# First weights held until the first tokens are normalised, the MLP's transposes spread between its last additions, and twice the buffers for its output rows

## The chip, the cores and the metric

The kernel runs on one core of one Trainium2 chip. The metric is the device time of one execution in microseconds (us), lower is better; the median of several runs is compared. The engines are TensorE (PE in the profile; PEld is its loading of weights), VectorE (DVE), ScalarE (ACT), GpSimd (POOL) and SyncE (SP), which issues the transfers (DMAs).

## The reference, cut to what matters

The input is one image of 48 x 48 positions ("tokens", 2304 in all) with 768 channels, float32. Two layers follow each other:

```python
# layer 0: a transformer block
xn  = layernorm(x);  q, k, v = xn @ qkv_w + qkv_b        # 12 heads of 64
attn = softmax(q k^T * scale + rel_h + rel_w);  x = x + (attn v) @ proj_w + proj_b
h = gelu(layernorm(x) @ mlp_w1 + mlp_b1);  x = x + h @ mlp_w2 + mlp_b2   # 768 -> 3072 -> 768
# layer 1: a spectral filter
xf = rfft2(x);  o = two small complex matrix products per frequency, 8 channel blocks of 96
x = irfft2(softshrink(...)) + x
```

## The kernel before, in words

Everything is float32. A tile of tokens is 128 tokens x 768 channels, so there are 18 tiles. The order of the work on TensorE is written out by hand in the kernel (`manual_schedule`), and in the first stage that of SyncE's transfers too; on VectorE, ScalarE and GpSimd a scheduler orders the instructions when the kernel is built, and each engine then works through its list in that order. Large matrix products are made by Strassen's scheme with seven products for eight, so there are sums of blocks of weights (`left` and `right`, on GpSimd, lines L152 to L161) and of tokens (`sums_of_tokens`, four subtractions on VectorE, L170).

**The start.** `queries_keys_values` works in three blocks of six tiles. For the first block, `arrive` issues six loads of tokens (L373, 384 KB each, 128 rows of 3,072 B), `normal` normalises each tile (`normalise`: two statistics L116, their combination L118, a square root on ScalarE L120, a reciprocal L121 and the scaling L124). Then `weights_of` issues the first two pairs of weights, two loads each (L357, 384 KB each in pieces of 512 B), and `left` prepares them on GpSimd. `channels_first` transposes the tiles on TensorE (L386) and reads the results by VectorE (L389) and ScalarE (L393) into the token block `xt`; `sums_of_tokens` makes `xs`; then the products of L429 begin.

**The MLP.** It goes through three blocks `p` of 768 tokens. For each block, twelve steps `n` make 256 hidden channels each (`hidden`, products of L958, Gelu L964, then the sums `hs` on VectorE, L152 to L155) and add their share of the output (`added`, products of L1022 and L1018 into the four banks `o0` to `o3`, each read at once by VectorE into `x1` or `acc`, L1026, L1020, L1034). `added` of step n runs between the parts of `hidden` of step n + 1; the last step's three additions stand alone. While a block is worked on, the next block's tiles are normalised into `hats` (`normalised`). At the boundary of two blocks the kernel calls `turned`, which transposes the six normalised tiles of the next block (L1069, 36 transposes into the banks `h0` to `h3`, three to a bank) and reads the twelve filled banks into `xt`, by ScalarE (L1072) and VectorE (L1076) in turn. Then come the last three additions with `sums_of_tokens` cut in pieces between them, and `rows_forward`.

**From the MLP to the spectral stage.** `rows_forward(p)` multiplies the finished rows by a Fourier matrix (L1045, 16 results `zp` in the banks `o0` to `o3`), copies each into a buffer `zt` by ScalarE and VectorE in turn (`balanced_copy`, L75 and L77; four buffers), and writes each to memory (L1051). After the third block the spectral stage loads its first frequencies `zi` (L914) and starts with the products `fp` (L1168), whose banks are those that `zp` had, and whose results `xf` are copied by L75 and L77 in turn.

Of the kernel before, what the change touches and what calls it, by code (L numbers as in the profile page):

```python
# [18 lines left out]
P = 128  # L19
# [4 lines left out]
NC = C // P  # L24
# [5 lines left out]
G = 384  # L30
NB = 8
BS = C // NB
CH = C // 2
KW = HW // 2 + 1
# [5 lines left out]
V_LN1G, V_LN1B, V_LN2G, V_LN2B, V_QB, V_KB, V_VB, V_B1 = 0, 6, 12, 18, 24, 30, 36, 42  # L40
# [4 lines left out]
def block_then_afno(  # L45
# [25 lines left out]
    nc = tc.nc  # L71

    def balanced_copy(i, dst, src):
        if i % 2:
            nc.scalar.copy(dst, src)  # L75
        else:
            nc.vector.tensor_copy(dst, src)  # L77
# [11 lines left out]
    def col(i):  # L89
        return vec[:, i : i + 1]  # L90
# [18 lines left out]
    xt = shared[:, : NC * TB].rearrange("p (c t) -> p c t", c=NC)  # L109
    xs = shared[:, NC * TB :].rearrange("p (k c t) -> p k c t", k=3, c=3)  # L110

    def normalise(pool, src, hat=None):

        stats = pool.tile([P, 2, 6], F32, name="stats")
        for i in range(2):
            nc.vector.bn_stats(stats[:, i, :], src[:, ts(i, C // 2)])  # L116
# [7 lines left out]
        nc.vector.tensor_scalar(hat, src, mv[:, 0:1], rstd, ALU.subtract, ALU.mult)  # L124
        return hat

    def transposed(psum, hats, dst, g, gcol, bcol, tag):
# [35 lines left out]
    def sums_of_tokens(xt, xs, piece=None):  # L163

        b11, b12, b21, b22 = (xt[:, ds(3 * i, 3), ts(j, G)] for i in range(2) for j in range(2))
        t1, t2, t4 = (xs[:, i] for i in range(3))
        steps = ((t1, b12, b11), (t2, b22, t1), (t4, b21, t2), (b12, b22, b12))
        for i, (dst, a, b) in enumerate(steps):
            if piece is None or piece == min(i, 2):
                nc.vector.tensor_tensor(dst, a, b, ALU.subtract)  # L170
# [16 lines left out]
    with ExitStack() as flag_scope:  # L187
# [11 lines left out]
        with ExitStack() as att:  # L199
# [115 lines left out]
            def queries_keys_values(qkv):  # L315
# [35 lines left out]
                        [wvs[:, i] for i in range(3)],  # L351
                    )

                def weights_of(pr, slot):
                    w, ws = pairs[slot]
                    for i in range(2):
                        nc.sync.dma_start(  # L357
                            out=w[:, :, i],
                            in_=qkv_w[:, ds(i * C + pr * P, P)].rearrange("(c p) f -> p c f", p=P),
                        )  # L360
                    left(
                        nc.gpsimd, w[:, 0:3, 0], w[:, 3:6, 0], w[:, 0:3, 1], w[:, 3:6, 1],
                        [ws[:, i] for i in range(3)],
                    )
                    return w, ws
# [3 lines left out]
                def arrive(g):  # L369
# [3 lines left out]
                        nc.sync.dma_start(out=x3[:, i], in_=blocks[g, i])  # L373
                    arrived[g] = x3

                def normal(t):
                    x3 = arrived[t // 3]
                    normalise(ln1, x3[:, t % 3], x3[:, t % 3])

                def channels_first(g):  # L380
                    x3 = arrived[g]
# [103 lines left out]
                    orders.append(work)  # L485

                pairs_left = [i for work in orders for kind, i in work if kind == 0]
                ahead = [weights_of(pairs_left.pop(0), i) for i in range(2)]
                slot = 0
                for p in range(T // TB):  # L490
                    for g in (2 * p, 2 * p + 1):
# [426 lines left out]
    with ExitStack() as mlp:  # L918
# [81 lines left out]
        def added(p, n, i):  # L1000

            h, hs, v, vs = kept[p, n]
            bank = [psum.tile([P, CH], F32, name=f"o{k}") for k in range(4)]
            if n == 0:
                acc[i] = upool.tile([P, CH], F32, name=f"acc{i}", bufs=1)
            a11, a12, s3, a22 = (
                h[:, f, ds(k * G + i * P, P)] for f, k in ((0, 0), (1, 0), (0, 1), (1, 1))
            )
            s1, s2, s4 = (hs[:, k, ts(i, P)] for k in range(3))
            b11, t3, b21, b22 = (v[:, f, ts(k, CH)] for f in range(2) for k in range(2))  # L1010
            t1, t2, t4 = (vs[:, k] for k in range(3))
            t = 2 * (p * 3) + i
            x11, x12, x21, x22 = (
                x1[:, t + 3 * j, ts(k, CH)] for j in range(2) for k in range(2)
            )

            def product(k, a, b, start, *into):
                nc.tensor.matmul(bank[k], a, b, start=start, stop=True, skip_group_check=not start)  # L1018
                for dst in into:
                    nc.vector.tensor_tensor(dst, bank[k], dst, ALU.add)  # L1020

            nc.tensor.matmul(bank[0], a11, b11, start=True, stop=True)  # L1022
            if n == 0:
                nc.vector.tensor_copy(acc[i], bank[0])
            else:
                nc.vector.tensor_tensor(acc[i], bank[0], acc[i], ALU.add)  # L1026
            product(1, s2, t2, True, acc[i])
            product(2, s3, t3, True, x22)
            product(3, s1, t1, True, x22)
            product(0, a12, b21, False, x11)  # L1030
            product(2, a22, t4, False, x21)
            product(3, s4, b22, False, x12)
            if n == n_f - 1:
                nc.vector.tensor_tensor(x21, x21, acc[i], ALU.add)  # L1034
                nc.gpsimd.tensor_tensor(x12, x12, acc[i], ALU.add)
                nc.gpsimd.tensor_tensor(x22, x22, acc[i], ALU.add)

        def rows_forward(p):

            for k in range(2):  # L1040
                for g in (2 * p, 2 * p + 1):
                    for a, parts in enumerate(((0,), (1, 2), (3, 4), (5,))):
                        zp = psum.tile([2 * 2 * KW, CH], F32, name="zp", tag=f"o{a}")
                        for b in parts:
                            nc.tensor.matmul(  # L1045
                                zp, rows_dft[:, b, :], x1[:, 3 * g + b // 2, ts(k, CH)],
                                start=(b == parts[0]), stop=(b == parts[-1]),
                            )
# [8 lines left out]
        def normalised(p, i):  # L1057

            t = 6 * p + i
            hats[i] = turn.tile([P, C], F32, name="hat2", tag="turn")  # L1060
            normalise(upool, x1[:, t, :], hats[i])
            nc.gpsimd.tensor_tensor(x1[:, t, :], x1[:, t, :], b2, ALU.add)

        def turned():
            for j in range(2):
                for c in range(NC):
                    tp = psum.tile([P, G], F32, name="tp2", tag=f"h{c % 4}")
                    for i in range(3):
                        nc.tensor.transpose(tp[:, ts(i, P)], hats[3 * j + i][:, ts(c, P)], ident)  # L1069
                    dst = xt[:, c, ts(j, G)]  # L1070
                    if c % 2:
                        nc.scalar.activation(  # L1072
                            dst, tp, AF.Identity, bias=col(V_LN2B + c), scale=col(V_LN2G + c)
                        )
                    else:
                        nc.vector.tensor_scalar(  # L1076
                            dst, tp, col(V_LN2G + c), col(V_LN2B + c), ALU.mult, ALU.add
                        )

        with tc.manual_schedule(engines={mybir.EngineType.PE}):  # L1080
            for p in range(T // TB):
                for n in range(n_f):
                    work = hidden(p, n)
                    for i in range(3):
                        next(work)
                        if n:
                            added(p, n - 1, i)
                    if p < 2 and 4 <= n < 10:
                        normalised(p + 1, n - 4)
                if p < 2:  # L1090
                    turned()
                for i in range(3):
# [315 lines left out]
```

## Time and profile before

| What | Value |
|---|---|
| Median of three runs | 2972.0 us (2969.34, 2972.0, 2973.16) |
| The profiled execution's own time | 2968.75 us |
| Its span in the profile | 2966.9 us |
| TensorE busy | 2901.3 us, 98% of the span |
| VectorE, ScalarE, GpSimd busy | 60%, 29%, 21% |
| TensorE's clock granted, mean | 0.996 of full speed |
| From the first transposes to `rows_forward`, first boundary | 1964.03 to 1990.45 us |
| The same, second boundary | 2317.47 to 2342.52 us |
| `rows_forward` of the third block | from 2684.73 us |
| First `fp` | 2704.24 us |

All times of the profile are microseconds from the start of the span. The span leaves out what lies around the program, 1.85 us in this execution. A busy TensorE is one with matmuls in flight; the times of its matmuls are modelled at their ends. A row of the timeline gives start, length, engine, line, operation, what is written and read, how many instructions are merged, and in brackets how long the engine had been idle before and what ended that. A row of the windows gives the stretch, its length, the busy time of PE, PEld, DVE, ACT and POOL, the granted clock of TensorE, the mean busy share of the 16 DMA engines and the GB/s that they moved.

### The profile page before, as it was taken

To read this page: it belongs to the slowest core of one execution; us is meant where nothing else is said; L and a number is where in the kernel's file an instruction comes from. 1 tells how busy PE (TensorE), PEld (TensorE's weight loads), DVE (VectorE), ACT (ScalarE), POOL (GpSimd) and SP (SyncE) were. 2 spreads that over 40 slices of the span, in tenths; PEclk is the share of its full clock that TensorE was granted. 3 is DMA by queue.
4 is the path that set the end of the run, shared out by engine and by line. 5 is a ranking of instruction groups with operands and counts; after the bars stand their busy time and mean duration, and the time that the engine had idled before them with its cause. 6 is when DMAs were issued, how large, how long until landed. Compare 5 with 4: busy or idle time off the path is not lost. (4 is left out here: it accounts for less than half of the span.)

```text
span 2966.9 us, 40951 instructions
## 1 busy us (share of the span) xinstructions
PE 2901.3 (98%) x15771; PEld 1763.4 (59%) x15771; DVE 1779.2 (60%) x2576; ACT 867.4 (29%) x1344; POOL 609.4 (21%) x564
## 2 busy tenths in 40 slices
PE   6999999999999999999999999999999999999998
PEld 4555655655556555555555555555555555557995
DVE  4343237677777777777723666675666566664443
ACT  1011125655555556555500111011111111111210
POOL 2303010000000000000043332343233223312441
PEclk9999999999999999999999999999999999999999
DMA  4423276172452616435242021122112211213235
GB/s 118 152 87 115 94 161 125 26 135 57 83 123 42 141 33 104 103 58 87 62 166 85 32 64 54 54 70 64 51 62 64 75 44 64 64 57 88 78 89 177
DMA packets 202818, 253.04 MB, mean 85 GB/s; under 512 B 21618, under 2 KB 180978, under 8 KB 201078
## 3 DMA queue, kind: packets, MB, share of 16 engines
q1 hardware_dynamic: 202614, 250.32, 33.2%
q8 instruction: 127, 2.08, 0.3%
q14 instruction: 77, 0.63, 0.1%
HBM read 136.40 MB, written 50.14 MB: 63 GB/s over the span
## 5 line engine op out<-in xcount | busy, mean ns | idle before, releaser
L607 DVE TENSOR_TENSOR acc<-acc,main 128x768 f32<-128x768 f32 x576 | 551.8, 958 | 202.0 <-ACT main L550 145.4
L550 ACT ACTIVATE main<-sp 128x768 f32<-128x768 f32 x648 | 522.1, 811 | 155.8 <-PE sp L546 148.6
L546 PE MATMUL sp<-terms,select 64*128 64x384 f32 x1296 | 412.1, 629 | 0.0
L1020 DVE TENSOR_TENSOR main<-o,main 128x384 f32<-128x384 f32 x540 | 298.8, 556 | 40.3 <-PE o L1018 1.8
L958 PE MATMUL h<-shared,w 128*128 128x384 f32 x864 | 296.7, 486 | 0.8 <-issue 0.8
L540 PE MATMUL sp<-shared 64*128 64x384 f32 x1296 | 266.4, 488 | 2.8 <-DVE o L440 2.2
L540 PE MATMUL sp<-qT,kT 64*128 64x384 f32 x1296 | 266.5, 487 | 0.0
L585 POOL TENSOR_TENSOR inverse<-inverse,rden 128x384 f32<-128x384 f32 x36 | 46.3, 1287 | 1029.0 <-DVE rden L582 961.6
L429 PE MATMUL m<-main 128*128 128x384 f32 x756 | 247.1, 488 | 5.5 <-DVE rstd L121 2.6
L958 PEld LDWEIGHTS h<-shared,w 128*128 128x128 f32 x864 | 164.4, 190 | 116.1 <-issue 2.3
L958 PE MATMUL h<-shared,w1s 128*128 128x384 f32 x648 | 226.6, 486 | 0.0
L555 PE MATMUL op<-main,shared 128*64 128x384 f32 x1296 | 221.3, 488 | 0.0
L555 PE MATMUL op<-main,v 128*64 128x384 f32 x1296 | 219.9, 488 | 0.0
L429 PEld LDWEIGHTS m<-main 128*128 128x128 f32 x756 | 142.7, 190 | 107.5 <-issue 8.1
L964 ACT ACTIVATE hT<-c,vec 128x384 f32<-128x384 f32 x108 | 66.4, 615 | 466.2 <-DVE c L970 466.0
L970 DVE TENSOR_TENSOR c<-h,u 128x384 f32<-128x384 f32 x108 | 60.1, 557 | 212.4 <-PE h L958 212.4
L1018 PE MATMUL o<-w,hT 128*128 128x384 f32 x432 | 175.0, 487 | 2.2 <-DVE mv L118 2.0
L1018 PE MATMUL o<-w2s,hs 128*128 128x384 f32 x432 | 174.9, 487 | 1.1 <-DVE hs L153 1.1
L546 PEld LDWEIGHTS sp<-terms,select 64*128 64x128 f32 x1296 | 125.3, 186 | 83.8
L958 PEld LDWEIGHTS h<-shared,w1s 128*128 128x128 f32 x648 | 123.1, 190 | 85.9
L152 POOL TENSOR_TENSOR w1s<-w 128x384 f32<-128x384 f32 x36 | 36.2, 1005 | 611.7 <-PE o L1018 452.6
L555 PEld LDWEIGHTS op<-main,v 128*64 128x64 f32 x1296 | 89.9, 138 | 107.0 <-issue 107.0
(150 smaller groups left out, 3921.6 us busy)
## 6 DMA issues: line engine op xcount, KB each, us to landing
w<-in_mlp_w_dram SPq DMA_DIRECT2D x72, 768.0 KB
terms<-col_parts SPq DMA_DIRECT2D x432, 72.0 KB
terms<-row_hi SPq DMA_DIRECT2D x216, 72.0 KB
terms<-row_lo SPq DMA_DIRECT2D x216, 72.0 KB
main<-in_qkv_w_dram SPq DMA_DIRECT2D x36, 384.0 KB
z<-zt SPq DMA_DIRECT2D x48, 150.0 KB
zo<-z SPq DMA_DIRECT2D x12, 600.0 KB
x<-in_x_dram SPq DMA_DIRECT2D x18, 384.0 KB
```

Of the source, the lines that this page charges most:

```text
L429: nc.tensor.matmul(bank, a[:, c, :], b[:, c, :], start=(first and c == 0), stop=(c == 2), skip_group_check=not first,)
L540: nc.tensor.matmul(sp[:, j, :G], kT[at, ts(kt, P)], qT[at, ts(c, G)], start=True, stop=False,)
L546: nc.tensor.matmul(sp[:, j, :G], select[at, a % 2], ready[pr, c][at, a // 2, b], start=False, stop=True,)
L550: nc.scalar.activation(p, sp[:, :, :G], AF.Exp, scale=HD**-0.5)
L555: nc.tensor.matmul(op[ts(j, 64)], v[:, kt0 + i, ts(j, 64)], ps[i][:, j, :], start=(kt0 + i == 0), stop=(kt0 + i == NT - 1),)
L585: nc.gpsimd.tensor_tensor(inverse, inverse, rden, ALU.add)
L607: nc.vector.tensor_tensor(acc, made[0] if kt == 1 else acc, p, ALU.add)
L958: nc.tensor.matmul(bank[i], a[:, c, :], b[:, c, :], start=(start and c == 0), stop=(c == 2), skip_group_check=not start,)
L964: nc.scalar.activation(h[:, i, ts(k, G)], src, AF.Gelu, bias=col(V_B1 + 2 * n + i))
L970: nc.vector.tensor_tensor(t, src, other, ALU.add)
L1018: nc.tensor.matmul(bank[k], a, b, start=start, stop=True, skip_group_check=not start)
L1020: nc.vector.tensor_tensor(dst, bank[k], dst, ALU.add)
```

## The change

Three parts. First, `normalise` hands back its last instruction (the scaling), and each of the first four weight loads is made to wait for one: both loads of the first pair for that of tile 3, both of the second for that of tile 4. Second, `turned` is cut in three pieces of four banks, one ahead of each of the last three additions; all its reads are ScalarE's, and `sums_of_tokens` is called after the additions in one piece. Third, `zt` gets eight buffers for four, and for the first two blocks ScalarE makes all its copies.

```diff
-    def normalise(pool, src, hat=None):
+    def normalise(pool, src, hat=None, made=None):
...
-        nc.vector.tensor_scalar(hat, src, mv[:, 0:1], rstd, ALU.subtract, ALU.mult)
+        last = nc.vector.tensor_scalar(hat, src, mv[:, 0:1], rstd, ALU.subtract, ALU.mult)
+        if made is not None:
+            made.append(last)
...
-                def weights_of(pr, slot):
+                def weights_of(pr, slot, behind=None):
                     w, ws = pairs[slot]
                     for i in range(2):
-                        nc.sync.dma_start(
+                        load = nc.sync.dma_start(
                             out=w[:, :, i],
                             in_=qkv_w[:, ds(i * C + pr * P, P)].rearrange("(c p) f -> p c f", p=P),
                         )
+                        if behind is not None:
+                            tc.add_manual_dep(load.ins, behind.ins.name, ...)
...
-                    normalise(ln1, x3[:, t % 3], x3[:, t % 3])
+                    normalise(ln1, x3[:, t % 3], x3[:, t % 3], normalised)
...
-                ahead = [weights_of(pairs_left.pop(0), i) for i in range(2)]
+                ahead = [weights_of(pairs_left.pop(0), i, normalised[3 + i]) for i in range(2)]
...
-                        zt = turn.tile([2 * 2 * KW, CH], F32, name="zt", bufs=4)
-                        balanced_copy(a, zt, zp)
+                        zt = turn.tile([2 * 2 * KW, CH], F32, name="zt", bufs=8)
+                        if p < 2:
+                            nc.scalar.copy(zt, zp)
+                        else:
+                            balanced_copy(a, zt, zp)
...
-        def turned():
-            for j in range(2):
-                for c in range(NC):
-                    tp = psum.tile([P, G], F32, name="tp2", tag=f"h{c % 4}")
-                    for i in range(3):
-                        nc.tensor.transpose(tp[:, ts(i, P)], hats[3 * j + i][:, ts(c, P)], ident)
-                    dst = xt[:, c, ts(j, G)]
-                    if c % 2:
-                        nc.scalar.activation(dst, tp, AF.Identity, bias=..., scale=...)
-                    else:
-                        nc.vector.tensor_scalar(dst, tp, ..., ALU.mult, ALU.add)
+        def turned(piece):
+            for i in range(4 * piece, 4 * piece + 4):
+                j, c = divmod(i, NC)
+                tp = psum.tile([P, G], F32, name="tp2", tag=f"h{i % 4}")
+                for k in range(3):
+                    nc.tensor.transpose(tp[:, ts(k, P)], hats[3 * j + k][:, ts(c, P)], ident)
+                nc.scalar.activation(xt[:, c, ts(j, G)], tp, AF.Identity, bias=..., scale=...)
...
-                if p < 2:
-                    turned()
                 for i in range(3):
-                    added(p, n_f - 1, i)
                     if p < 2:
-                        sums_of_tokens(xt, xs, i)
+                        turned(i)
+                    added(p, n_f - 1, i)
+                if p < 2:
+                    sums_of_tokens(xt, xs)
                 rows_forward(p)
```

In the built order on the engines, the transfers of SyncE keep their sequence up to the end of the MLP. On VectorE the `L170` subtractions of a boundary stand after the second addition's evictions and among the third's; at the first boundary two L124, two L118 and two L116 of the block after next stand between the first and the second addition's evictions or among the second's. On ScalarE, at the first boundary, a table load and two square roots stand between the eighth and the ninth read of the transposes.

More of the change, by code (lines that the diff above doesn't have):

```diff
@@ L360, in weights_of @@
                         )
+                        if behind is not None:
+                            tc.add_manual_dep(
+                                load.ins, behind.ins.name,
+                                mybir.DependencyInfo(
+                                    mybir.DependencyClass.Sync, mybir.DependencyReason.DATA
+                                ),
+                                reason="tokens first",
+                            )
                     left(
@@ L374, in arrive @@
                     arrived[g] = x3
+                normalised = []
                 def normal(t):
                     x3 = arrived[t // 3]
-                    normalise(ln1, x3[:, t % 3], x3[:, t % 3])
+                    normalise(ln1, x3[:, t % 3], x3[:, t % 3], normalised)
                 def channels_first(g):
@@ L1062, in normalised @@
             nc.gpsimd.tensor_tensor(x1[:, t, :], x1[:, t, :], b2, ALU.add)
-        def turned():
-            for j in range(2):
-                for c in range(NC):
-                    tp = psum.tile([P, G], F32, name="tp2", tag=f"h{c % 4}")
-                    for i in range(3):
-                        nc.tensor.transpose(tp[:, ts(i, P)], hats[3 * j + i][:, ts(c, P)], ident)
-                    dst = xt[:, c, ts(j, G)]
-                    if c % 2:
-                        nc.scalar.activation(
-                            dst, tp, AF.Identity, bias=col(V_LN2B + c), scale=col(V_LN2G + c)
-                        )
-                    else:
-                        nc.vector.tensor_scalar(
-                            dst, tp, col(V_LN2G + c), col(V_LN2B + c), ALU.mult, ALU.add
-                        )
+        def turned(piece):
[4 more added lines that the diff above has]
+                    nc.tensor.transpose(tp[:, ts(k, P)], hats[3 * j + k][:, ts(c, P)], ident)
+                nc.scalar.activation(
+                    xt[:, c, ts(j, G)], tp, AF.Identity, bias=col(V_LN2B + c), scale=col(V_LN2G + c)
+                )
         with tc.manual_schedule(engines={mybir.EngineType.PE}):
@@ L1089, in block_then_afno @@
                         normalised(p + 1, n - 4)
+                for i in range(3):
+                    if p < 2:
+                        turned(i)
+                    added(p, n_f - 1, i)
                 if p < 2:
-                    turned()
-                for i in range(3):
-                    added(p, n_f - 1, i)
-                    if p < 2:
-                        sums_of_tokens(xt, xs, i)
+                    sums_of_tokens(xt, xs)
                 rows_forward(p)
```

## The prediction

> **What bounds the kernel now.** I read the engines' shares first, to see which engine a gain has to come from.
>
> ```profile
> PE 2901.3 (98%) x15771; PEld 1763.4 (59%) x15771; DVE 1779.2 (60%) x2576; ACT 867.4 (29%) x1344; POOL 609.4 (21%) x564
> ```
>
> TensorE is idle for only 2966.9 - 2901.3 = 65.6 us. No instruction of it is removed, so a gain is idle time, or matmuls that ran at a lower clock. The waits of TensorE (what waited, for what: sum, times, longest) say where:
>
> ```profile
> PE m L386 <- DVE x L124: 15.5, 3, 14.5
> ...
> PE tp L1069 <- DVE shared L1076: 6.4, 3, 3.0
> ...
> PE fp L1168 <- ACT zt L75: 3.9, 1, 3.9
> ```
>
> The first is the kernel's start, the second the two boundaries between the MLP's blocks, the third the step from the MLP to the spectral stage. The change touches these three and nothing between. Then windows: engines' busy times, granted clock, DMA share, GB/s.
>
> ```profile
> 4.00:8.00 4.00, 0.00 (x0) 0.00 (x0) 0.86 (x2) 0.00 (x0) 0.00 (x0) 1.00 0.53 170
> 8.00:11.00 3.00, 0.00 (x0) 0.00 (x0) 1.14 (x4) 0.29 (x1) 0.00 (x0) 1.00 0.86 179
> ...
> 65.00:69.00 4.00, 4.00 (x14) 2.41 (x13) 1.02 (x2) 0.00 (x0) 3.88 (x4) 1.00 0.50 201
> ```
>
> The last row is a token load with nothing beside it: 201 GB/s. From 8 to 11 us tokens and weights together move 179. The next view is the timeline of the start:
>
> ```profile
> 17.45 0.56 DVE L116 BATCH_NORM_STATS2 stats<-x 128x6 f32<-128x384 f32 x1 [0.82 <-DMA x<-in_x_dram]
> ...
> 20.27 0.56 DVE L116 BATCH_NORM_STATS2 stats<-x 128x6 f32<-128x384 f32 x1 [1.62 <-DMA x<-in_x_dram]
> 20.74 0.67 DVE L124 TENSOR_SCALAR x<-x,mv,rstd 128x768 f32<-128x768 f32 x1
> ...
> 29.31 6.75 DVE L170 TENSOR_TENSOR main<-main 128x1152 f32<-128x1152 f32 x4
> ```
>
> VectorE waits for the tokens: the sixth tile arrives at 20.27, and all behind it up to the first sums (29.31) is a chain. Second boundary, timeline:
>
> ```profile
> 2317.80 1.47 PE L1069 MATMUL tp<-ident,hat 128*128 128x128 f32 x12
> ...
> 2322.28 0.87 PE L1069 MATMUL tp<-ident,hat 128*128 128x128 f32 x6 [3.01 <-DVE shared L1076]
> ...
> 2342.81 15.67 PE L1045 MATMUL zp<-main,rows_dft 128*100 128x384 f32 x48
> ```
>
> Four banks of transposes are written in 1.5 us; then TensorE waits until VectorE, busy with `hs` (L152 to L155), reads the first. Last, the end of the MLP in the chain of waits, and its clock in the windows:
>
> ```profile
> 2697.96 5.68 DMA z<-zt
> ...
> 2703.71 0.49 ACT zt L75
> ...
> 2704.24 5.31 PE fp L1168 x32
> ```
> ```profile
> 2700.40:2704.20 3.80, 0.00 (x0) 0.00 (x0) 0.56 (x1) 0.48 (x1) 0.00 (x0) 0.77 0.89 271
> 2704.20:2709.50 5.30, 5.26 (x32) 5.13 (x32) 1.11 (x2) 0.47 (x1) 0.00 (x0) 0.52 0.64 201
> ```
>
> The last `zt` copies wait for one of four buffers to be written out; then 32 matmuls run at a clock of 0.52.
>
> [...] 3.87 us idle, then 0.52; and 0.53 from 1968.8 to 1972.2, in the transposes after the 3.0 us wait. [...] weight packets (512 B) run among token packets (3,072 B) from 8 us on. [...] an L170 took 1.35 us alone and 2.28 beside GpSimd's L1062. [...] table loads stand only before Sqrt and Gelu, so more reads on ScalarE add none.
>
> **A, the start: 3.7 us.** Each of the first four weight loads gets a wait on an L124 (which `normalise` now hands back, with no instruction more): pair 0 on that of tile 3, pair 1 on that of tile 4. On VectorE the L124 of tile 3 (20.74) stands behind the first statistics of tile 5, so the weights start when the last token has landed. What it gains: in the trace's DMA records 33 token packets start per half microsecond when alone (65 to 69 us; 121 ns each), and 17 to 21 beside weights (200 to 250 ns each). 217 of 768 packets had started by 8 us; the other 551 at 66 per us take 8.35 us: the last lands at 16.5 in place of 19.6, 3.1 us earlier. The slower pace from 5.5 us on begins as the weights' issue does (5.77), so counted from 5.5 us (85 packets) it is 683 / 66 = 10.35, 15.9: 3.7 earlier. I take 3.7. VectorE needs some 2.1 us a tile against an arrival each 1.94, so it keeps step, and L170 starts at 25.6. What it costs: SP stands at the wait, with nothing behind it before L441 (39.69). GpSimd's `left` and the first product wait for the weights. L124 of tile 3 ends at 17.7; later pairs took 5.6 us from issue to L152 (45.92 to 51.52; 59.47 to 65.04): 23.3, where it was 22.65. TensorE's first product wants them at 25.7, the second wants L153 (25.7) but also the second L170 (25.6 + 3.5 = 29.1). So 2.4 us are spare. Bounds: 0 (the tokens' pace has another cause) to 4.2; the clock's warm-up, which the trace shows from 30 us on, could shift by one window (1.7 us of loss).
>
> **B, the two boundaries: 4.2 + 5.2 us.** Moved: 36 transposes in pieces of 12 before each of the last three additions; their 12 reads all go to ScalarE (0.67 us each); VectorE loses 6 reads (4.0 us) and, for p < 2, 8 `zt` copies (4.5 us); the L170s come after the reads. In the second boundary TensorE took from 2317.47 to 2342.52, 25.05 us. Its work there: 36 transposes at 0.109 (12 in 1.47) = 3.9, and three additions of 4.52 (2675.38 to 2679.90 in the last block) = 13.6: 17.5. Afterwards, step by step: piece 1 ends at 2319.1. Addition 1 waits for `hs` (L155 ends 21.2) and for its first eviction L1026 behind it: ends 2324.5, not 23.6. Piece 2 and addition 2: 1.3 + 4.5, 2330.4. Piece 3: 2331.7. In addition 3 VectorE has 8 evictions at 0.525 and two L170 of 1.35 in between, 6.9 us, the first L170 held until ScalarE has read the ninth bank: ends about 2337.3. Gain 5.2. ScalarE's 4 reads (2.7 us) have the 4.5 us of an addition as cover; without that cover each later piece would wait up to 1.4 us. The first boundary (1964.03 to 1990.45, 26.4 us) has more on VectorE: in the order of instructions two L124, two L118 and two L116 (2.6 us) stand among addition 2, L1062 slows an L170 by 0.9; I count 4.2. There ScalarE also gets a table load (1.28) and two Sqrt between the eighth and ninth read, done some 2 us before the ninth bank is full. Bounds: 1 and 3 (VectorE as late as now) to 7 and 7.5 (no wait left). 16 `zt` copies on ScalarE, 7.7 us, lie beside 15.6 us of matmuls: no cost; if they fell behind, TensorE would wait for bank `o`.
>
> **C, the end of the MLP: 5.5 us.** With eight `zt` buffers the last copies need only their matmul: 0.2 + 0.48 us after 2700.4, so `fp` starts 0.75 us later instead of 3.87: 3.1 us. Its frequencies (`zi`) are there: by the packets, 192 for the first unit are through by 2699.6. No idle window, so the 32 matmuls run at full clock: 8 take 0.68 there, 32 take 2.7; with the `xf` copies 2.9 in place of 5.3: 2.4 us. Bounds 3.1 (clock still low) to 5.9. The four more buffers cost space only.
>
> **Sum.** 3.7 + 4.2 + 5.2 + 5.5 = 18.6 us off the profiled execution: span 2948.3, time 2968.75 - 18.6 = 2950.2. The median of the runs is 3.25 above that execution, so 2972.0 - 18.6 = 2953.4.
>
> **Rivals.** (1) The tokens do not come earlier: weight packets may use DMA engines that had no tokens left. [...] Against: a packet's 121 ns growing to 250. A is then 0: 2957. (2) VectorE becomes the bound in all three additions: for: 18.31 us busy of 18.6 after the first transposes; against: it loses 8.5 us of work there. B then gives 4.5: 2958. (3) C fails, because `zi` or the `xf` copies end last: for: the DMAs are 0.89 busy there; against: the packets. C gives 1: 2958. (4) Slower: the held weights arrive late. Place: TensorE's first L429. Price: a microsecond for each that they land past 25.7 us. From 44.3 us (25.7 + the 18.6 gained) on the whole is slower than before, from 50.2 by over 0.2%: 2978 or more. It would take a wait that is not met until later VectorE work; nothing in the order shows one.
>
> **How the numbers follow.** Forecast 0.58, (1) 0.19, (2) 0.13, (3) 0.07, (4) 0.03. The forecast's own bounds, two or three of them met together, reach 11 to 23 us; with the rivals at 14 to 15, the range is 2948.5 to 2961. 0.2% is 5.9 us, about what a measurement of this kernel tells from no change; every case but (4) is beyond it, unless two rivals meet: faster 0.93, same 0.04, slower 0.03.
>
> **What would show it.** Right: the sixth token's statistics at about 16.5 us and L170 at 25.6; no wait of transposes for a read above 1 us, and 19 to 22 us from the first transposes to the first `zp`; `fp` within 1 us of the last `zp`, at clock 1.0. Wrong: L170 still after 28; waits of L1018 for L1020 over 4 us a boundary; `fp` waiting for `zi`.

## The result, and the profile after

The changed kernel's first four runs took 2962.34, 2953.37, 2949.14 and 2953.81 us, median 2953.59, against 2972.3 for the kernel before beside it: a ratio of 0.9937 (95% interval 0.9918 to 0.9957), 18.7 us less. The forecast was 2953.4. That the two agree within 0.2 us is luck: the four runs spread over 13 us. Two later groups of six runs each, with their own runs of the kernel before, gave 2955.32 (ratio 0.9945, 0.9929 to 0.9961) and 2952.94 (0.9935, 0.9921 to 0.9949).

The sum came out. The first trace of the changed kernel, though, seems to say that a fifth of it is wrong. It is the trace of the run of 2962.34 us, the longest of the four (span 2960.5). Its engines' shares, then TensorE's waits (sum, times, longest):

```profile
PE 2902.6 (98%) x15771; PEld 1762.2 (60%) x15771; DVE 1768.2 (60%) x2548; ACT 881.1 (30%) x1372; POOL 610.2 (21%) x564
```
```profile
PE m L398 <- DVE x L124: 15.8, 2, 14.7
...
PE m L441 <- DVE main L172: 2.9, 2, 1.7
...
PE fp L1178 <- ACT zt L75: 0.6, 1, 0.6
```

The wait of the transposes for their reads (6.4 us before) has no row any more, and that of `fp` fell from 3.9 to 0.6. But the start's wait (L398, which was L386) is as long as it was, 15.8 for 15.5. (Lines below L124 moved: L170 is now L172, L429 is L441, L1069 is L1085, L1045 is L1057, L1018 and L1020 are L1030 and L1032, L1168 is L1178.) The windows of the start, with the DMA share and GB/s as the last two columns, and VectorE's timeline:

```profile
4.00:8.00 4.00, 0.00 (x0) 0.00 (x0) 0.71 (x2) 0.00 (x0) 0.00 (x0) 1.00 0.51 151
8.00:11.00 3.00, 0.00 (x0) 0.00 (x0) 1.44 (x4) 0.29 (x1) 0.00 (x0) 1.00 0.52 139
```
```profile
18.51 0.56 DVE L116 BATCH_NORM_STATS2 stats<-x 128x6 f32<-128x384 f32 x1 [1.19 <-DMA x<-in_x_dram]
...
21.24 0.56 DVE L116 BATCH_NORM_STATS2 stats<-x 128x6 f32<-128x384 f32 x1 [1.53 <-DMA x<-in_x_dram]
...
29.83 8.00 DVE L172 TENSOR_TENSOR main<-main 128x1152 f32<-128x1152 f32 x4
```

No weights run here before 22.4 us, and still the tokens move at 139 to 151 GB/s: the sixth tile came at 21.24 (20.27 before), the sums at 29.83 (29.31 before), and they took 8.00 us for 6.75. By this trace step A lost a microsecond. The second boundary and the end of the MLP, timeline of TensorE:

```profile
2318.46 1.47 PE L1085 MATMUL tp<-ident,hat 128*128 128x128 f32 x12
...
2325.41 1.47 PE L1085 MATMUL tp<-ident,hat 128*128 128x128 f32 x12
...
2331.24 1.47 PE L1085 MATMUL tp<-ident,hat 128*128 128x128 f32 x12
...
2336.90 0.91 PE L1030 MATMUL o<-w2s,hT 128*128 128x384 f32 x2 [0.95 <-DVE main L1032]
...
2338.58 3.71 PE L1057 MATMUL zp<-main,rows_dft 128*100 128x384 f32 x11
```
```profile
2696.69 3.32 PE L1178 MATMUL fp<-shared,zi 96*96 96x96 f32 x32 [0.57 <-ACT zt L75]
```
```profile
2696.70:2700.00 3.30, 3.18 (x32) 2.85 (x32) 1.11 (x2) 0.47 (x1) 0.00 (x0) 1.00 0.74 245
```

Three pieces of twelve transposes, each 1.47 us without a gap; 20.1 us from the first to `zp`, which had been 25.0. The 32 `fp` take 3.32 us at clock 1.00, where they took 5.31 at 0.52 after 3.87 us of idling.

This one execution was only 6.4 us shorter than the traced one of before (2962.34 for 2968.75). From the first transposes (or the first `zp`) to what follows, it gained 2.4, 4.9 and 5.3 us at the three places; it lost 1.0 at the start, some 1.7 by windows at half clock (granted 0.50, 3.4 us each) at 87.1 and 431.9 us that the trace of before lacks, and some 3 at the end, where another pair of such windows lies at 2940.7 (0.50 for 6.8 us). So the first question is whether the hold fails, or whether this execution is not typical.

### The profile page after: what moved, and what is told of

Its sections match the earlier page's. It is cut to its first block, busy times and chain, and to the rows that moved or that the text cites. A ratio compares the mean times of both kernels' runs of the same rounds, so it can differ in the third digit from the quotient of the medians.

```text
span 2960.5 us, 40962 instructions
## 1 busy us (share of the span) xinstructions
PE 2902.6 (98%) x15771; PEld 1762.2 (60%) x15771; DVE 1768.2 (60%) x2548; ACT 881.1 (30%) x1372; POOL 610.2 (21%) x564
## 5 line engine op out<-in xcount | busy, mean ns | idle before, releaser
L1032 DVE TENSOR_TENSOR main<-o,main 128x384 f32<-128x384 f32 x540 | 299.4, 556 | 41.0 <-PE o L1030 2.1
L441 PE MATMUL m<-main 128*128 128x384 f32 x756 | 248.4, 490 | 6.2 <-DVE main L172 2.9
L441 PEld LDWEIGHTS m<-main 128*128 128x128 f32 x756 | 143.4, 191 | 108.7 <-issue 10.1
L1030 PE MATMUL o<-w,hT 128*128 128x384 f32 x432 | 175.2, 487 | 3.7 <-DVE mv L118 2.0
L1030 PE MATMUL o<-w2s,hs 128*128 128x384 f32 x432 | 174.9, 487 | 1.4 <-DVE hs L155 1.3
L552 PEld LDWEIGHTS sp<-shared 64*128 64x128 f32 x1296 | 117.7, 187 | 60.3 <-issue 23.1
```

Source lines behind the costliest of these rows:

```text
L441: nc.tensor.matmul(bank, a[:, c, :], b[:, c, :], start=(first and c == 0), stop=(c == 2), skip_group_check=not first,)
L552: nc.tensor.matmul(sp[:, j, :G], kT[at, ts(kt, P)], qT[at, ts(c, G)], start=True, stop=False,)
```

## The experiments

Twelve sets of runs, of ten kernels, came in four groups, each with its own runs of the kernel before. "The second product" is the second group of products L441 (L429 before), the first that waits for a token sum: where it starts, the whole start is paid. Packets per us are counted from the trace's DMA records; a packet of a token load is one row of 3,072 B.

### Group 1: the parts alone

**No hold** (the changed kernel without its first part):

```diff
-                ahead = [weights_of(pairs_left.pop(0), i, normalised[3 + i]) for i in range(2)]
+                ahead = [weights_of(pairs_left.pop(0), i) for i in range(2)]
```

> The changed kernel without the wait of the first four weight loads: the spread transposes and the eight buffers alone. Theory (the hold gives nothing, since the changed kernel's own trace had its first token sums L172 at 29.83 us, where the kernel before had 29.31): 18 to 21 us faster than before, about 2952, level with the changed kernel or up to 3 us faster; the sixth token's statistics at 20.3 us, the first sums at 29.3, and no wait of the second product for the last L172. Rival (the prediction's step A, a hold that gains 3.7 us, which one profiled execution may have hidden): 3 to 4 us slower than the changed kernel, about 2957. The losses in the profiled execution at half-clock windows at 87, 432 and 2941 us belong to that execution and not to the change: they need not return here; if they return at the same places, they belong to the spread or the buffers.

Measured: 2958.11, ratio 0.9954 (0.9940 to 0.9968), so 13.7 us (9.5 to 17.8) below before. Its first sums came at 28.49, its second product at 32.06: earlier than in the first trace of the changed kernel (29.83, 33.84), yet its times are longer than three of that kernel's four runs. The windows at half clock came back at 86.3 and 431.0 us. No part of the change brings them each time: the kernel with the spread alone had them at 85.7 and 430.4, and the third trace of the changed kernel, with all three parts, had neither. All four traces with this pair are of kernels with the spread, though, so it is not shown that the spread plays no part.

**Hold only** (the kernel before with the first part of the change alone):

> The kernel before with the hold of the first weights alone. Theory (the tokens' pace does not come from the weights): sixth token's statistics at 20.3 to 21.3 us, first sums at 29.3 to 30, weights issued at 22.4, second product about 1 us later than before because GpSimd's sums then lie beside the four token sums; time 0 to 3 us above before. Rival (step A of the prediction): statistics at 16 to 17 us, sums at 25.6, time 3 to 4 us below before.

Measured: 2968.82, ratio 0.9994 (0.9985 to 1.0002), between 4.5 us less and 0.6 more than before. Its trace shows the lower pace as well: 156 and 147 GB/s from 4 to 8 and from 8 to 11 us, statistics of the sixth tile at 20.51, sums at 29.10. Trace and time pull apart again, and the interval holds both theories.

**Buffers only** (the kernel before, `bufs=8`):

```diff
-                        zt = turn.tile([2 * 2 * KW, CH], F32, name="zt", bufs=4)
+                        zt = turn.tile([2 * 2 * KW, CH], F32, name="zt", bufs=8)
```

> The kernel before with eight buffers for zt alone. Theory (step C): the first fp starts within 1 us of the last zp at clock 1.0; from the first zp of the third block to the first lp 20 us for 25.4; time 5 us below before. Rival (C's gain in the changed kernel came from the other parts, by another phase of the clock's windows): the wait of fp falls by 3 us but the clock stays near 0.5, so 3 us; or fp then waits for zi, 1 us.

Measured: 2967.49, ratio 0.9984 (0.9974 to 0.9995), 4.8 us less. Timeline and window of the first `fp`:

```profile
2700.17 3.31 PE L1168 MATMUL fp<-shared,zi 96*96 96x96 f32 x32 [0.57 <-ACT zt L75]
```
```profile
2699.60:2704.00 4.40, 3.20 (x32) 2.87 (x32) 1.10 (x2) 1.43 (x3) 0.00 (x0) 1.00 0.77 268
```

The wait is 0.57 and the clock 1.00: 20.1 us from the first `zp` to the first `lp` for 25.4. The buffers alone do the whole of C.

**Spread only** (the kernel before with the pieces, ScalarE's reads, and ScalarE's `zt` copies for p < 2, four buffers):

> The kernel before with the transposes in three pieces, all their reads on ScalarE, and zt copied by ScalarE in the first two blocks, with the four buffers of before. Theory (step B as the changed kernel's trace sizes it): first boundary 24 us for 26.4, second 20 for 25.05, so 7 to 8 us faster; the step to the spectral stage as before (25.4 us). Rival (the boundaries' gain needs the eight buffers, since ScalarE's copies would wait for a free zt): 4 us or less, with TensorE waiting in rows_forward. Rival (B as predicted): 9.4 us.

Measured: 2964.25, ratio 0.9974 (0.9965 to 0.9983), 7.7 us less. Boundaries 23.0 and 20.2 us for 26.4 and 25.0; the step to the spectral stage 25.5, as before. The eight buffers are not needed for B. The interval (5.1 to 10.4 us) does not tell this size from the 9.4 of the prediction.

### Group 2: the same kernels again, and the hold elsewhere

**The changed kernel again:**

> The changed kernel again, for a second trace of its start and more times. The start's traces so far disagree with its times: with the hold the tokens came at 45 to 48 packets per us in both traced executions (175 to 190 ns each), no faster than without it, but at an equal mean clock the other executions with the hold are some 4 us shorter than those without. Theory (two paces: the six token loads together run either at 66 or at 45 packets per us, and the two traced executions fell on the slow one): this trace, or the next with a hold, shows 60 to 68 packets per us, the last token at 16 to 17 us and the first L172 near 26; time 3 to 5 us below the kernel without the hold. Rival (the hold gives nothing): packets at 45 to 48 again, L172 at 29 to 30, and the time within 2 us of the kernel without the hold.

Measured: 2955.32, ratio 0.9945. From 7 us on the trace has 66 to 69 packets per us, all at 121 ns; the last token landed at 15.6 us, the first L172 started at 23.67, the second product at 27.90. The theory of more than one pace held.

**No hold again** (same edit as in group 1):

> The changed kernel without the hold of the first weights, again, beside the changed kernel on one chip. Theory (the hold gains in most executions): 3 to 5 us slower than the changed kernel; weights' bursts from 8 us on, tokens at 40 to 45 packets per us beside them, L172 at 28 to 29.5. Rival (the hold gives nothing): level with the changed kernel within 2 us.

Measured: 2960.59, ratio 0.9961 (0.9946 to 0.9976): 5.3 us slower than the changed kernel beside it, with overlapping intervals. This trace fell on the lower pace, with the weights between:

```profile
23.14 0.56 DVE L116 BATCH_NORM_STATS2 stats<-x 128x6 f32<-128x384 f32 x1 [2.24 <-DMA x<-in_x_dram]
...
32.85 5.96 DVE L172 TENSOR_TENSOR main<-main 128x1152 f32<-128x1152 f32 x4
```

The sixth tile's statistics came at 23.14, its second product at 36.41. The two traces with the hold at the lower pace had it at 33.84 and 32.93, some 3 us earlier. But for a gain at the lower pace this one trace speaks alone: the kernel before and buffers only, which ran between the paces before any weights moved (50 and 52 packets per us from 5.5 to 7.7 us, here 46), had it at 32.88 and 32.63.

**Hold three tiles earlier:**

```diff
-                ahead = [weights_of(pairs_left.pop(0), i, normalised[3 + i]) for i in range(2)]
+                ahead = [weights_of(pairs_left.pop(0), i, normalised[i]) for i in range(2)]
```

> The changed kernel with each hold three tiles earlier: the first pair's loads behind the scaling of tile 0, the second's behind that of tile 1. The weights start at about 9 to 11 us, so GpSimd's sums end before the four L172, which then take 6 to 6.8 us for the 8.0 of the changed kernel's trace, and the wait of the second product for L172 is 1 us and not 1.7. Theory (what the hold gains is the tokens' pace before the weights start, and what it costs is GpSimd's sums beside L172): the weights' packets then share the engines with tiles 4 to 6; between the kernel without the hold and the changed kernel, 0 to 2 us above the latter. Rival (the pace of the tokens is the same with and without weights): 1 us faster than the changed kernel, by the shorter L172.

Measured: 2953.27, ratio 0.9944 (0.9927 to 0.9960), level with the changed kernel. At the higher pace the weights' packets started at 13.8 us and delayed the last tile to 16.4; the four L172 took 6.76 us from 26.46 on, and the second product started at 30.03. That is 2.1 us after the changed kernel at the same pace (27.90) and 1.6 to 2.0 before the two traces without the hold at that pace (31.60, 32.06), as the theory had it. The sixth tile's statistics came 1.4 us later (17.42 for 16.00), and from there to the first L172 another 1.4 us went, in part beside GpSimd, where one L124 took 1.12 us for 0.67. The shorter sums don't make up for both. The times did not resolve these 2 us.

**Reads on both engines in turn, place kept:**

```diff
-                nc.scalar.activation(
-                    xt[:, c, ts(j, G)], tp, AF.Identity, bias=..., scale=...)
+                dst = xt[:, c, ts(j, G)]
+                if c % 2:
+                    nc.scalar.activation(dst, tp, AF.Identity, bias=..., scale=...)
+                else:
+                    nc.vector.tensor_scalar(dst, tp, ..., ALU.mult, ALU.add)
```

> The changed kernel with the reads of the spread transposes on VectorE and ScalarE in turn, as in the kernel before: what of step B is the place, and what the engine that reads. VectorE gets six reads of 0.67 us back in each boundary, in front of each addition's evictions. Theory (VectorE is what the boundary waits for, busy 18.3 of 18.6 us in the kernel before): 24 for 20 us in the second boundary and 26 to 27 for 23.6 in the first, so 6 to 8 us slower than the changed kernel; the gain of B is mostly the engine. Rival (the gain is the place, since the reads lie beside matmuls wherever they are made): 1.3 us a boundary or less (two reads ahead of the first eviction of each addition), under 3 us in all.

Measured: 2956.76, ratio 0.9950 (0.9934 to 0.9967). Boundaries 22.9 and 20.2 us, no wait more. My theory fell: the six reads (4.0 us of VectorE's time a boundary) went back to VectorE, and the boundaries are as short. In time this kernel is 1.4 us behind the changed one, which the intervals do not resolve.

### Groups 3 and 4: start once more, and what of B is needed

**The changed kernel, third time:**

> The changed kernel a third time, for a trace of its start and as the measure for the two others on this chip. Theory (two paces of the token loads, each execution falls on one): either 66 to 68 packets per us, last token at 16 us, first L172 at 23.5 to 24.5 us, or 45 to 48 packets per us and L172 at 29 to 30; nothing between for all six loads. Time 2953 to 2957 us, 15 to 19 below before.

Measured: 2952.94, ratio 0.9935. Windows and VectorE's timeline of the start:

```profile
4.00:8.00 4.00, 0.00 (x0) 0.00 (x0) 1.02 (x2) 0.00 (x0) 0.00 (x0) 1.00 0.50 180
8.00:11.00 3.00, 0.00 (x0) 0.00 (x0) 1.55 (x5) 0.59 (x2) 0.00 (x0) 1.00 0.51 206
```
```profile
16.46 0.56 DVE L116 BATCH_NORM_STATS2 stats<-x 128x6 f32<-128x384 f32 x1 [0.51 <-DMA x<-in_x_dram]
...
24.49 7.59 DVE L172 TENSOR_TENSOR main<-main 128x1152 f32<-128x1152 f32 x4
```

206 GB/s, where the first trace of the same program had 139, at DMA shares of 0.51 and 0.52. The sixth tile's statistics start at 16.46; the prediction said about 16.5.

**Hold two tiles earlier** (`normalised[1 + i]`):

> The changed kernel with each hold two tiles earlier: the first pair's loads behind the scaling of tile 1, the second's behind that of tile 2 (at the fast pace 12.8 and 13.9 us, where the hold on tile 0 came to 12.3 and that on tile 3 to 17.2). Theory (the hold's cost is that GpSimd's sums lie beside the four L172, 8.0 to 8.2 us for 6; its gain is the tokens' pace up to their last packet at 15.8): weights' packets start at 15 to 15.5, the last token lands no later than 16.3, GpSimd starts at 20.5 to 21, the four L172 take 7 to 7.5 us, and the second product starts 0.5 to 1 us before that of the changed kernel at the same pace (27.9 us); time 0 to 1 us below it. Rival (the weights' packets cost the last tile as much as they spare GpSimd): level or 1 us above. A pace of 45 to 48 would say nothing on either.

Measured: 2955.61, ratio 0.9940 (0.9925 to 0.9954), level. The pace was 54 to 58 packets per us, at 126 to 150 ns for most, so "nothing between" is wrong, and on where best to hold the weights this trace says nothing: the pace outweighs it. The second product started at 32.15.

**Place only** (reads on both engines in turn, and the `zt` copies as before):

```diff
-                        if p < 2:
-                            nc.scalar.copy(zt, zp)
-                        else:
-                            balanced_copy(a, zt, zp)
+                        balanced_copy(a, zt, zp)
```

> The changed kernel with the place of the transposes alone of step B: their reads on VectorE and ScalarE in turn, and the zt copies of the first two blocks on both engines in turn, as in the kernel before. Theory (the place is the whole gain of B; moving work from VectorE to ScalarE gives nothing): boundaries of 22.9 to 24 us and 20.2 us, as with the changed kernel, no new wait of TensorE in rows_forward, and a time within 2 us of the changed kernel. Rival (the moved zt copies are what keeps VectorE in step): TensorE waits in rows_forward or in the first steps of the next block, 2 to 4 us slower.

Measured: 2964.06, ratio 0.9971 (0.9959 to 0.9982), against 0.9935 of the changed kernel on the same chip: 11 us of the gain gone. TensorE's waits, then the timelines of TensorE and VectorE at the second boundary:

```profile
PE zp L1057 <- DVE zt L77: 5.8, 3, 2.3
```
```profile
2335.13 4.03 PE L1057 MATMUL zp<-main,rows_dft 128*100 128x384 f32 x12
2341.41 11.86 PE L1057 MATMUL zp<-main,rows_dft 128*100 128x384 f32 x36 [2.25 <-DVE zt L77]
```
```profile
2337.47 3.42 DVE L172 TENSOR_TENSOR shared<-shared 128x1152 f32<-128x1152 f32 x2
2340.82 1.01 DVE L77 COPY zt<-zp 100x384 f32<-100x384 f32 x2
```

The boundary up to `zp` is as short as ever (20.4 us). But VectorE ends it with two L172 still to do, 3.42 us; the `zt` copies stand behind them, the four banks are full after twelve matmuls, and TensorE waits 2.25 us. The rival was right in its mechanism, and its 2 to 4 us were too few. From the first boundary to the end of the MLP this trace is 6.3 us longer than the third of the changed kernel, which is all but 0.1 of what the two traced executions differ by. But it is the shortest of its eight runs (2960.29); what the others lost beyond it was not located.

**`zt` on both engines, reads on ScalarE** (the diff of the kernel above, in the changed kernel):

> The changed kernel with one edit taken back: the zt copies of the first two blocks are made by ScalarE and VectorE in turn again; the reads of the spread transposes stay ScalarE's. Theory (the copies on VectorE stand behind the L172 that are left at the end of the additions, and bank o waits for them): with no reads on VectorE only one or two L172 (1.35 to 2 us) are left after the last eviction, where the kernel with reads on both engines had two (3.42 us) and TensorE waited 2.25 us for a zt copy at each boundary; so a wait of 0.5 to 1.5 us at each boundary, 1 to 3 us slower than the changed kernel, about 2956 to 2958. Rival (the copies alone decide, whatever reads the transposes): 2.2 us of wait at each boundary again and a time as of that kernel, about 2964. Rival (ScalarE's reads make up for it): no wait, level with the changed kernel, 2953 to 2956.

Measured: 2953.87, ratio 0.9941 (0.9924 to 0.9958), level. One L172 is left at the end of the second boundary, and the wait behind it is shorter; at the first boundary there is none:

```profile
2331.04 2.15 DVE L172 TENSOR_TENSOR shared<-shared 128x1152 f32<-128x1152 f32 x1
2333.12 1.01 DVE L77 COPY zt<-zp 100x384 f32<-100x384 f32 x2
```
```profile
PE zp L1057 <- DVE zt L77: 1.0, 1, 1.0
```

The theory held at one boundary alone, and in time the rival "level" did. So the place with one relief of VectorE, of the reads or of the copies, gives the gain of B, and the second relief adds nothing that shows. The place with neither shortens the boundaries and loses the time again behind them: 8.6 us less than before in all, where the hold (1.8 to 4.4, see below) and the buffers (4.8) account for 6.6 to 9.2. The relief without the place was not run.

### What sets the tokens' pace

In all these starts the mean DMA share is 0.50 to 0.53 while tokens move alone, at 139 GB/s as at 206. The products of packets per us and duration say the same of both paces: 66 x 121 ns and 45 x 187 ns are both about 8 packets at a time. The same rows of 3,072 B are loaded again before the projection, there as 128 rows in one sequence. Window of the changed kernel's first trace:

```profile
1439.70:1447.10 7.40, 7.40 (x50) 3.27 (x46) 4.87 (x6) 2.34 (x3) 0.00 (x0) 1.00 0.88 317
```

317 GB/s at a share of 0.88: 103 packets per us, at 136 ns in the mean, are 14 at a time. The loads of the start take each tile as 8 rows of the image with 16 positions each. So the share was 0.50 to 0.53 with tiles in this shape and 0.88 with 128 rows in one sequence. That the shape is the cause was not shown: no run loaded the first tokens in another one. Why some eight packets at a time took 121 ns each in one execution and 187 in the next stays open. It differed between executions of one program, with no weights in sight.

## Why the prediction was right, point by point

**A, 3.7 us: the size held, by another sum, and the first trace was the misleading one.** Start of the second product in all traced executions but the two with the hold placed earlier (30.03 and 32.15):

| Kernels | Start of the second product, us | Mean |
|---|---|---|
| No hold: before, no hold (twice), buffers only, spread only | 32.88, 32.06, 36.41, 32.63, 31.60 | 33.1 |
| Hold behind tiles 3 and 4: changed (three), hold only, reads in turn, place only, `zt` on both | 33.84, 27.90, 28.09, 32.93, 28.45, 27.71, 27.78 | 29.5 |

The difference of the means is 3.6 us. By the times, the changed kernel's 16 runs have a mean of 2954.6 and the ten without the hold 2959.0: 4.4 us, with a standard error of 1.4 (spread of the runs; several chips). But the rows of the table mix the paces. Five of seven with the hold, and two of five without (no hold for the first time, spread only), ran at 55 packets per us or more from 5.5 to 7.7 us, when no weights moved in any of them; so a part of the difference can be chance. At this higher pace alone it is 28.0 for 31.8, 3.8 us. At the lower pace it is 33.4 for the one 36.4.

At the higher pace the mechanism can be read. Without the hold the tokens ran at 64 to 66 packets per us (121 ns) until the weights' first packets at 8.1 to 8.2 us, and then at 48 to 49 (188 ns) up to 11 us; with it they ran at 67 to 68 in the same stretch. So rival (1), tokens no earlier, is out there, though two of seven traced executions with the hold look just like it.

The sum inside A is another than predicted. The sixth tile's statistics came 2.8 us earlier at this pace (16.1 for 18.9, means), where 3.7 was counted; against the traced execution of before (20.27), which ran between the paces, it is 4.1, and part of that is the pace. From there to the first sums the traces without the hold took 9.4 us and those with it 8.1, a gain of 1.3 that the prediction did not have. Two scalings of tokens and the second product without the hold (its first trace), then one scaling and the second product with it (second trace of the changed kernel):

```profile
21.12 1.43 DVE L124 TENSOR_SCALAR x<-x,mv,rstd 128x768 f32<-128x768 f32 x1
...
23.78 1.00 DVE L124 TENSOR_SCALAR x<-x,mv,rstd 128x768 f32<-128x768 f32 x1
...
32.06 28.30 PE L441 MATMUL m<-main 128*128 128x384 f32 x87 [1.22 <-DVE main L172]
```
```profile
20.20 0.67 DVE L124 TENSOR_SCALAR x<-x,mv,rstd 128x768 f32<-128x768 f32 x1
...
27.90 32.57 PE L441 MATMUL m<-main 128*128 128x384 f32 x95 [1.89 <-DVE main L172]
```

Without the hold GpSimd's first sums lay beside the last scalings, one or two of which took 1.00 to 1.46 us; the hold moves the sums behind them, and each takes 0.67. Where the clock came up too late to matter, this alone accounts for the stretch: 8.6 us with no slow scaling (three traces with the hold), 9.0 with one, 9.7 with two. In the other four traces with the hold, all at the higher pace, the clock helped too: it came up at 21.9 to 23.2 us, and the last transposes then followed each other every 0.11 us for 0.21 before (without the hold it came up at 27.7 us or later).

GpSimd's sums then lie beside the four L172, which is the cost that the prediction left out ("2.4 us are spare" counted only when the weights arrive): 7.6 to 8.2 us with the hold behind tile 3, 6.0 to 6.75 without it. The second product waits for two of the four and paid 0.2 us for it at the higher pace (3.6 to 4.2 us behind the first L172, for 3.6). So 3.7 came out partly by luck: the tokens gave less than counted, and GpSimd and the clock made up for it. The reading that raised 3.1 to 3.7, that the tokens' slower pace from 5.5 us on was the weights', does not hold: in the trace of before the first packet of weights starts at 7.8 us, and the tokens' pace from 5.5 to 7.7 us differed as much with the hold (45 to 68) as without it (46 to 66). (The prediction's packet times are 0.2 us late against the span: 233 packets had started by 8 us, not 217. The differences that it takes from them stand.)

**B, 4.2 + 5.2 us: right in the second boundary, a size off in the first.** The second went from 25.0 to 20.1 us, a gain of 4.9. The first went from 26.4 (one window at half clock inside, 0.53 from 1968.8 to 1972.2 us) to 23.0 without such a window and 24.0 with one: 2.4 to 3.4 for 4.2. The mis-sized term is VectorE's work beside GpSimd: in the first trace a pair of L124 took 2.16 us there (1.22 at the start), two L172 took 2.15 each (an L170 alone 1.35), and L1030 waited 0.67 and 1.28 us for L1032. Rival (2), VectorE as the bound in all three additions, came in part at most: beside these waits the second boundary has one of 0.95 us, no piece of transposes waited, and 7.3 to 8.3 us of gain are far from its 4.5. What B had wrong is how much of its working was needed. It counted on the place (reads under an addition's matmuls) and on 8.5 us of work taken off VectorE, the reads and the copies. The experiments show that half of the second is enough: either relief with the place gives the gain, and the place with neither loses some 6 us behind the boundaries. "No cost" for the moved `zt` copies held. The reading of the table loads missed one, ahead of the attention's Exp (L550, at 430.97 us of the trace of before); their number stayed at ten, so the reads on ScalarE added none, as forecast.

**C, 5.5 us: held.** 5.3 us, in every kernel with eight buffers, 0.57 us of wait and clock 1.00 (3.87 and 0.52 before). Rival (3) is out. Rival (4), late weights, did not occur: at the higher pace they landed by 24.0 to 24.6 us and GpSimd began at 22.6 (third trace); at the lower they landed at 28.5 and 29.6, and the second product still waited for L172.

**The sum.** 3.6 + 2.9 + 4.9 + 5.3 = 16.7 us from the traces' stages, taking 2.9 as the middle of the first boundary; 18.7 from the first four runs, 16.3 and 19.3 from the ratios of the later groups. The forecast of 18.6 is within what these leave open. By the times the parts run alone give 1.8 + 7.7 + 4.8 = 14.3 us. The part that falls short is the hold, 1.8 alone (0.6 more to 4.5 less) for 4.4 in the changed kernel. Within their errors the two agree; whether it is worth less alone stays open.

## What to carry to other kernels

When one traced execution contradicts the times, look at the same stage in several executions before dropping the mechanism: here the pace of the first loads moved the start by 6 us from one execution to the next, more than the hold gained. Compare executions of one pace, too: a mean over a few of them can be the mix of paces. When transfers are held back, follow the work that waits for them to its new neighbours: GpSimd's sums left VectorE's scalings (1.00 to 1.46 us beside the sums, 0.67 alone) and landed beside its subtractions (7.6 to 8.2 us for 6.0 to 6.75). Place work whose results are needed late (transposes into banks that must be read) between matmuls that need other banks, rather than asking first for a faster reader (here 20.1 to 20.4 us for 25.0 at the second boundary, with the reads on one engine as on two), and then check what is left in the queue of the engine that was postponed: it stands in front of the next stage's copies (here two L172, 3.42 us, and a wait of 2.25). For a load that something waits for, compare the DMA share with 1: here a share of half, with several loads outstanding, went with tiles taken as 8 rows of 16 positions, and 0.88 with 128 rows in one sequence.

## What the runs showed of the hardware that was not expected

- One program's first six loads ran at 45 packets per us (187 ns each) in one execution and at 66 to 69 (121 ns) in others, with 54 to 58 (126 to 150 ns) between in a close variant.
- A scaling on VectorE (L124, 128x768, one tile in and one out) took 0.67 us alone and 1.00 to 1.46 beside GpSimd's sums; of those, each 128x384 sum took 1.0 us alone and 2.1 beside L172.
- In the clock records of the trace of before and of the changed kernel's first, each window at half clock (granted 0.50) begins a whole number of steps of 3.413 us after the moment at which the clock first comes up (29.8 and 29.1 us): in the latter the first two came 17 steps (58.0 us) and 118 steps (402.8 us) after it. The changed kernel's first trace had six single ones and a pair before its last 10 us, its third trace two and a pair. By its length and clock a window can cost 1.7 us where TensorE is busy (an estimate: half of 3.413). So part of the spread of the runs of one kernel (2960 to 2980 us in 40 runs of before) may be which gaps happen to meet the grid: a guess, which no experiment tested.
- Windows that were not empty were followed by one at half clock. In the trace of before TensorE was busy for 0.63 us of the 3.4 from 1965.2 us and for 0.88 of the 3.4 from 2320.2 us, with waits of 2.96 and 3.01 us that begin in or just before them; the next window ran at half clock both times (0.53 from 1968.8 us, 0.50 from 2323.6).
